# Selective-scan and attention kernel: five residual parts, stores over two blocks, one lasting tile for the scans of two states

## The chip, the cores and the metric

The kernel runs on one core of a Trainium2 chip. The metric is the device time of one execution in microseconds (us), the median of three runs. TensorE is called PE in the profile, VectorE DVE, ScalarE ACT, GpSimd POOL; SP is the SyncE queue, which issues DMAs only. ACT and POOL issue DMAs as well as computing.

## The reference, cut to what matters

There are 16 images of 128 channels by 64x64 positions, thus 4096 tokens each. Layer 0 is a selective scan with two channel halves of 128 and 16 states:

```python
def step(hs, inp):                      # over the 4096 tokens of an image
    d_t, B_t, C_t, u_t = inp
    dA = jnp.exp(d_t[:, :, None] * A)
    h_new = dA * hs + (d_t * u_t)[:, :, None] * B_t[:, None, :]
    y_t = jnp.einsum('bdn,bn->bd', h_new, C_t)
    return (h_new, y_t)
...
x = x + _L0_conv_ref(_gn(x), ...)       # the residual of layer 0
t = _to_tokens(x)
t = t + _L1_attn_ref(_ln_t(t), W_kv, q_proj)
t = t + _L1_ffn_ref(_ln_t(t), gate_w, gate_b, weight1, weight2)
```

Layer 0 has a grouped normalisation, an input projection, a causal convolution of four taps, the scan, a gate and an output projection; its result is added to its input `x`. Layer 1 has a causal attention with one query per head, and a mixture of experts.

## The kernel before, in words

**Blocks and steps.** An image is cut into 8 blocks of 512 tokens (`L = 512`, `NBLK = 8`). The first and longest stage is one loop over `k` (L804): iteration k runs the scan of block k, prepares block k+1 (normalise, convolution, projections, `delta`), finishes block k-1 (gate, output projection), and runs the attention of block m = k-9, nine blocks behind. Here i is the block's place in its image (0 to 7). An iteration has 16 steps, one for each state n (L873).

**What a step does.** DVE multiplies `bx = du * B` for both halves (`product`, two instructions), copies the last column of the scan of the step before into `state` (`keep_state`, one small reduction; left out in an image's last block), and runs the two scans (`scan`), each over 512 tokens. POOL multiplies the scan's result by C into `da` (`product_c`), one step behind DVE, and for n = 1, 3, 5, 7 issues a DMA that adds the product of the state before (`add_pair`, `da<-da`). PE sums the products in PSUM by transposes (`add_y`, names `y0` to `y13`; `yp14`, `yp15` run in the next iteration). SP loads `bct`, the rows of B and C spread to 128 partitions, three steps ahead (`load_bc`, five buffers). ACT makes the decays `da = exp(delta * a)` (`d`).

**The order written out by hand.** All else is placed by the table `STEP` (L749): for each step three lists of names, which run before the scans, between the two scans, and after them. Each engine executes its own instructions in that program order, and each engine issues its DMAs in its own order. The names that matter below: `k0`-`k7` and `v0`-`v7` are attention keys and values (a PE product, taken out by ACT with Silu); `s0`, `s1` scores on PE; `mx`, `l0`-`l5` the running maximum of the scores on DVE, `sexp` its exponential; `store` (ACT) writes the scores' logarithms to DRAM as `pd<-parts`, 96 KB in rows of 128 bytes, and `spread` (SP) reads them back in ten small DMAs (`lh<-pd`, `rh<-pd`), for the weights `w0`; `bcs` (ACT) stores B and C of the next block; `cen`, `sq`, `var`, `lnsc`, `la` are the token normalisation (`la` is DVE's `xn<-cen_ps,rstd`); `g0`, `g1` the gate on DVE (`z<-y_ps,z`); `gnl` loads and `gs` reduces a block of a later image (`stats<-xs`); `fin0`, `fin1` store the attention's result (`t_d<-tx`); `put` (ACT) copies a block of layer 0's result into `xt`, which holds one whole image (`res[b]`, one buffer).

**The residual.** When an image's last block has been put (iteration with i = 0 of the next image), POOL adds `x` to `xt` by DMA (`ar0`-`ar3`, `xt<-in_x_dram`, an accumulating DMA on POOL's queue), and ACT stores the sum to DRAM in quarters of 512 KB (`sr0`-`sr3`, `t_d<-xt`). The attention reads it from there block by block (`lx0`, `lx1`), but for the first block, which `cen` reads from `xt` directly.

After this loop come a gating stage, the experts and a final addition, which the change does not touch.

Of the kernel before, what the change touches and what calls it, by code (L numbers as in the profile page):

```python
# [8 lines left out]
F32 = mybir.dt.float32  # L9
BF16 = mybir.dt.bfloat16  # L10
AF = mybir.ActivationFunctionType
ALU = mybir.AluOpType
# [3 lines left out]
P = 128  # L16
L = 512
# [22 lines left out]
def bc(ap, shape):  # L40

    return ap.to_broadcast(list(shape))
# [3 lines left out]
def conv_attn_hybrid(ctx: ExitStack, tc: tile.TileContext, x, w_in, conv_w, conv_b, w_xproj, w_dt, b_dt,  # L46
                     a_log, d_param, w_out, w_kv, q_proj, gate_w, gate_b, weight1, weight2, out):
    nc = tc.nc
    NB, C, HH, WW = x.shape
    T = HH * WW  # L50
    NBLK = T // L
# [4 lines left out]
    NH2 = DI // P  # L56
# [11 lines left out]
    x_f = x.rearrange("b c h w -> b c (h w)")  # L68
# [19 lines left out]
    with ExitStack() as st:  # L88
# [5 lines left out]
        PE, DVE, ACT, POOL, SP = (InOrder(tc, e) for e in (nc.tensor, nc.vector, nc.scalar, nc.gpsimd, nc.sync))  # L94
# [131 lines left out]
        mp = st.enter_context(tc.tile_pool(name="mp", bufs=2))  # L226
        m1 = st.enter_context(tc.tile_pool(name="m1", bufs=1))
        dap = st.enter_context(tc.tile_pool(name="dap", bufs=13))
        hp_ = st.enter_context(tc.tile_pool(name="hp", bufs=2))
        bcp = st.enter_context(tc.tile_pool(name="bcp", bufs=5))  # L230
        tmp = st.enter_context(tc.tile_pool(name="tmp", bufs=6))
        vp_ = st.enter_context(tc.tile_pool(name="vp", bufs=4))
# [5 lines left out]
        blocks, gn, res, att = {}, {}, {}, {}  # L238

        def load_exp():  # L240
            tc.keep_in_program_order(nc.scalar.preload_act_table_set(EXP_LN))  # L241
# [4 lines left out]
        def bank(name):  # L246
            return ps.tile([P, L], F32, tag="ps", name=name)
# [16 lines left out]
        def gn_end(b, part):  # L264

            w = gn[b]
            if part == 0:
                w["mv"] = stp.tile([P, 2], F32, tag="mv", name="mv")
                w["gs"] = stp.tile([P, 5], F32, tag="gs", name="gs")
                DVE.bn_aggr(w["mv"], w["stats"].rearrange("p a b -> p (a b)"))  # L270
            mv, gs = w["mv"], w["gs"]
            if part == 1:
                w["gp"] = bank("gn_ps")
                PE.matmul(w["gp"][:, 0:1], gmat, mv[:, 0:1], start=True, stop=True)
                ACT.copy(gs[:, 0:1], w["gp"][:, 0:1])
            if part == 2:
                far = w["gp"][:, 1:2]
                DVE.tensor_tensor(far, mv[:, 0:1], w["gp"][:, 0:1], ALU.subtract)
                DVE.scalar_tensor_tensor(gs[:, 1:2], far, far, mv[:, 1:2], ALU.mult, ALU.add)
            if part == 3:  # L280
                w["gp"] = bank("gn_ps2")
                PE.matmul(w["gp"][:, 0:1], gmat, gs[:, 1:2], start=True, stop=True)
                ACT.activation(gs[:, 2:3], w["gp"][:, 0:1], AF.Ln, bias=eps)
                ACT.activation(gs[:, 3:4], gs[:, 2:3], AF.Exp, scale=-0.5)
            if part == 4:
                DVE.tensor_scalar(gs[:, 4:5], gs[:, 0:1], gs[:, 3:4], -1.0, ALU.mult, ALU.mult)
# [22 lines left out]
        def conv(k, a, taps=range(KC)):  # L309

            w = blocks[k]
            if taps[0] == 0:
                w[f"xs{a}"] = bank("xs_ps")
            pt = w[f"xs{a}"]
            for t in taps:
                PE.matmul(pt, wc[:, t, bass.ts(a, P)], w["xb"][:, t : t + L], start=(t == 0), stop=(t == KC - 1))
# [79 lines left out]
        def scan(k, n, between):  # L396


            w = blocks[k]
            b, i = w["b"], w["i"]  # L400
            if n == 0 and i == 0:
                gn[b]["state"] = stp.tile([P, N, NH2], F32, tag="state", name="state")
            bt, da, bx = w.pop(("bc", n)), w["da", n], w.pop("bx")
            h = w["h", n] = hp_.tile([P, NH2, L], F32, tag="h", name="h")
            for a in range(NH2):
                if a:
                    between(n)
                DVE.tensor_tensor_scan(h[:, a, :], da[:, a, :], bx[a],
                                       0.0 if i == 0 else gn[b]["state"][:, n, a : a + 1], ALU.mult, ALU.add)
            w["hc", n] = bt  # L410
# [15 lines left out]

        def keep_state(k, n):
            w = blocks[k]
            h = w.pop(("h", n))
            if w["i"] < NBLK - 1:  # L430
                DVE.tensor_reduce(gn[w["b"]]["state"][:, n, :], bc(h[:, :, L - 1 :], [P, NH2, 2]),
                                      mybir.AxisListType.X, ALU.max)

        def add_y(k, n):

# [39 lines left out]

        def add_residual(b, part):

            cols = (slice(0, L), slice(L, 2 * L), slice(2 * L, 4 * L), slice(4 * L, T))[part]
            for a in range(cols.start, cols.stop, 4 * L):
                to = slice(a, min(a + 4 * L, cols.stop))  # L480
                POOL.dma_start(res[b][:, to], x_f[b, :, to], accum_op=ALU.add)

        def store_residual(b, part):
            ACT.dma_start(t1_d[b, :, bass.ts(part, T // 4)], res[b][:, bass.ts(part, T // 4)])
# [152 lines left out]
        def split(m, part):  # L637
            s = att[m]
            ACT.copy(s["parts"][:, part], s["rest"][:, :P].rearrange("p (w s) -> p w s", s=64))
# [99 lines left out]
        def finish(m, f):  # L739
# [7 lines left out]
        PAIRS = (1, 3, 5, 7)  # L747
        LEAD, LEAD_BC = 8, 3
        STEP = (  # L749
# [16 lines left out]
        )  # L766
        order = [(k, n) for k in range(NK) for n in range(N)]
        made = 0
# [35 lines left out]
        for k in range(NK + LAG + 1):  # L804
            b, i = divmod(k, NBLK)
            cur = k if k < NK else None
            prev = k - 1 if 0 <= k - 1 < NK else None
# [9 lines left out]
                norm=(nxt, norm_block), conv0=(nxt, lambda k: conv(k, 0)), conv1=(nxt, lambda k: conv(k, 1, range(KC // 2))),  # L817
                conv2=(nxt, lambda k: conv(k, 1, range(KC // 2, KC))), csilu=(nxt, conv_silu), xproj=(nxt, xproj),
                bcs=(nxt, store_bc), delta=(nxt, delta), z=(cur, gate_silu), skip=(cur, skip),
                
                outp=(prev, out_proj), put=(prev, put_back),
                cen=(mn, ln_center), sq=(mn, ln_square), var=(mn, ln_var), lnsc=(mn, ln_scale), 
                mx=(m, score_max), sexp=(m, score_exp), tsc=(m, turn_scores), ssum=(m, score_sum),
                ssp=(m, spread_scores), slog=(m, score_log), rest1=(m, lambda m: rest(m, 1)), split1=(m, lambda m: split(m, 1)),
                rest2=(m, lambda m: rest(m, 2)), split2=(m, lambda m: split(m, 2)), store=(m, store_parts),
                spread=(m, spread_parts), inv=(m, inverse), lx0=(mn, lambda m: load_x(m, True)), lx1=(m, load_x),
                gnl=(stat, lambda s: gn_load(*s)),
                lb=(k + 2 if k + 2 < NK else None, lambda k: load_block(k, ACT)),
                nt=(k + 2 if k + 2 < NK else None, no_tokens), exp=(0, lambda _: load_exp()))
# [27 lines left out]
                ops[f"yp{n}"] = (prev, lambda k, n=n: add_y(k, n))  # L857
            for part in range(5):
                ops[f"ge{part}"] = (ends, lambda b, part=part: gn_end(b, part))
            for part in range(4):  # L860
                ops[f"ar{part}"] = (b - 1 if i == 0 and prev is not None else None, lambda b, part=part: add_residual(b, part))
                ops[f"sr{part}"] = (b - 1 if i == 0 and prev is not None else None, lambda b, part=part: store_residual(b, part))

            def do(n, part):
                for name in STEP[n][part].split():
# [34 lines left out]
    with ExitStack() as st:  # L900
        PE, DVE, ACT, POOL, SP = (InOrder(tc, e) for e in (nc.tensor, nc.vector, nc.scalar, nc.gpsimd, nc.sync))
# [17 lines left out]
        gn = rp_.tile([E, C], F32, name="gn", bufs=1)  # L919
# [145 lines left out]
        for it in range(NIT + LATE + 2):  # L1065
            p, i = divmod(it, NBLK)
# [22 lines left out]
            last, left = divmod(it - LATE - 2, NBLK)  # L1089
# [6 lines left out]
    with ExitStack() as st:  # L1096
# [3 lines left out]
        hp = st.enter_context(tc.tile_pool(name="hp", bufs=2))  # L1100
# [7 lines left out]
        for e0 in range(0, E, EG):  # L1108
            w1 = wpool.tile([P, EG, HID], F32, tag="w1", name="w1")
# [17 lines left out]
            ops = ps.tile([P, O], F32, tag="ops", name="ops")  # L1127
# [12 lines left out]
    with ExitStack() as st:  # L1140
        ps = st.enter_context(tc.tile_pool(name="cps", bufs=4, space=PSUM))
        cp = st.enter_context(tc.tile_pool(name="cp", bufs=2))
        for pr in range(NB // 2):
# [4 lines left out]
            for j in range(2):  # L1148
                b = 2 * pr + j
                t = cp.tile([P, T], F32, tag=f"t{j}", name=f"tc{j}")  # L1150
# [34 lines left out]
```

## Time and profile before

| | us |
|---|---|
| median of 3 runs | 9472.11 (9468.96 to 9473.5) |
| the profiled execution | 9471.73 |
| its span, first to last instruction | 9470.0 |
| busy: PE / DVE / ACT / POOL | 8291.2 / 8447.0 / 7282.9 / 5899.4 |
| DVE scans, 4096 of 512 columns | 4993.5 |
| DVE products `bx`, 4096 | 2652.0 |
| DVE `state<-h`, 1792 | 283.1 |
| mean granted TensorE clock | 0.933 |

The profile shows one execution. A group's row ends with: count | busy us, mean ns of one | idle time of that engine just before them, and what ended it. A row of waits has: who waited <- for what: us in total, times, longest. A row of a timeline has: start, length, engine, line, operation, count, and in brackets the idle time before it. Line 37 is the helper through which all instructions of the loop pass, so groups are told apart by the names of their tiles. Buffer numbers are left out. Rows of DMAs on POOL's queue carry a time to landing; on SP's and ACT's queues they do not, and landings there are read from what waited for them. Neighbouring DVE instructions overlap in the timeline: an instruction's length reaches some 0.1 us past the start of the next one.

### The profile page before, as it was taken

Reading aid. Unit: us, or ns where it says so; the run is one execution under the profiler, and the core shown is the slowest. Engines: PE = TensorE matmul, PEld = TensorE weight load, DVE = VectorE, ACT = ScalarE, POOL = GpSimd, SP = SyncE. Lnnn points to the kernel's source line nnn. Section 1 sums busy time; section 2 is a strip of 40 time slices with the busy share of each in tenths; the row PEclk is TensorE's granted clock in tenths of the full one; section 3 lists DMA queues with packets and bytes.
Section 4 is the critical chain, followed back from the end, with each engine's and each line's share of the span. In section 5 each row is a group of like instructions: output and inputs, shape, how many; then the busy total and the mean of one; then the engine's idle time right before and its main releaser. Section 6 shows DMA issues by size and latency. Waiting matters only on the chain.

```text
span 9470.0 us, 189268 instructions
## 1 busy us (share of the span) xinstructions
PE 8291.2 (88%) x69596; PEld 5233.9 (55%) x69596; DVE 8447.0 (89%) x13057; ACT 7282.9 (77%) x13950; POOL 5899.4 (62%) x2683
## 2 busy tenths in 40 slices
PE   5679999999989999999999999999999999877775
PEld 3446555555555565555555555555565555545642
DVE  8999999999999999999999999999999999603733
ACT  5568888888888888888888888888888888755730
POOL 6777777777777777777777777767777777500000
PEclk7789999999999999999999999999999999998976
DMA  6777877778777777777877777777877777502358
GB/s 173 184 201 189 202 193 201 191 196 204 189 203 193 201 189 203 192 198 197 201 191 196 200 190 202 195 197 190 202 194 199 197 196 189 147 22 71 113 183 358
DMA packets 978050, 1783.75 MB, mean 188 GB/s; under 512 B 194953, under 2 KB 275489, under 8 KB 967905
## 3 DMA queue, kind: packets, MB, share of 16 engines
q1 hardware_dynamic: 715264, 1347.76, 51.2%
q0 software_dynamic: 82944, 302.03, 16.2%
q10 hardware_dynamic: 178912, 121.86, 4.1%
q8 instruction: 548, 8.98, 0.4%
q14 instruction: 382, 3.12, 0.1%
HBM read 1363.99 MB, written 138.94 MB: 159 GB/s over the span
## 4 chain that ended last, share of the span: by engine, by line
PE 34%; ACT 20%; DMA 17%; DVE 15%; issue 8%; POOL 5%; SPq 1%; ACTq 0%; POOLq 0%; DVEq 0%
DVE h L37 8%; ACT da L37 7%; PE k_ps L37 6%; DMA da<-da 6%; PE y_ps L37 5%; PE v_ps L37 5%; POOL da L37 5%; DMA bct<-bcs 5%; PE ao_ps L37 4%; DVE bx L37 4%; PE xs_ps L37 3%; DMA pd<-parts 3%; PE s_ps L37 2%; ACT L37 2%; DMA xs<-in_x_dram 2%
## 5 line engine op out<-in xcount | busy, mean ns | idle before, releaser
L37 POOL TENSOR_TENSOR da<-h,bct 128x1024 f32<-128x1024 f32 x2048 | 5432.5, 2653 | 2155.8 <-DVE bx L37 1249.7
L37 DVE TENSOR_TENSOR_SCAN h<-da,state,bx 128x512 f32<-128x512 f32 x3584 | 4398.3, 1271 | 0.0
L37 DVE TENSOR_TENSOR bx<-du,bct 128x512 f32<-128x512 f32 x4096 | 2652.0, 698 | 60.4 <-DMA bct<-bcs 60.3
L37 ACT ACTIVATE da<-delta,a_neg 128x512 f32<-128x512 f32 x4096 | 2610.4, 717 | 15.4 <-DMA bct<-bcs 7.5
L37 PE MATMUL y_ps<-ident,da 128*128 128x128 f32 x12288 | 1698.8, 293 | 383.6 <-POOL da L37 219.2
L37 PEld LDWEIGHTS y_ps<-ident,da 128*128 128x128 f32 x12288 | 1515.1, 152 | 593.9 <-POOL da L37 257.8
L37 PE MATMUL v_ps<-wv,xn 128*64 128x512 f32 x4096 | 1032.4, 610 | 37.9 <-ACT tx L37 28.8
L37 ACT ACTIVATE v<-v_ps 128x512 f32<-128x512 f32 x1024 | 613.9, 600 | 526.4 <-PE v_ps L37 388.9
L37 PE MATMUL xs_ps<-xb,wc 128*128 128x512 f32 x2048 | 967.8, 606 | 2.5 <-issue 1.8
L37 PE MATMUL k_ps<-xn,wk 128*128 128x512 f32 x2048 | 951.1, 607 | 0.0
L37 ACT ACTIVATE kt<-k_ps 128x512 f32<-128x512 f32 x1024 | 612.6, 598 | 340.8 <-PE k_ps L37 270.7
L37 PEld LDWEIGHTS k_ps<-xn,wk 128*128 128x128 f32 x2048 | 369.6, 190 | 488.4 <-issue 435.4
L37 PE MATMUL ao_ps<-v,wm 128*64 128x128 f32 x8192 | 578.2, 285 | 54.9 <-ACT wm L37 54.8
L37 DVE TENSOR_TENSOR_SCAN h<-da,bx 128x512 f32<-128x512 f32 x512 | 595.2, 1203 | 0.0
L37 PEld LDWEIGHTS ao_ps<-v,wm 128*64 128x64 f32 x8192 | 451.7, 140 | 222.1 <-ACT wm L37 82.4
L37 POOL DMA_DIRECT2D da<-da x512 | 449.3, 878 | 163.4 <-POOL da L37 153.4
L37 PEld LDWEIGHTS xs_ps<-xb,wc 128*128 128x128 f32 x2048 | 368.2, 195 | 326.7 <-issue 325.7
L37 ACT ACT_TABLE_LOAD x397 | 509.4, 1283 | 21.6 <-issue 8.6
L37 PEld LDWEIGHTS v_ps<-wv,xn 128*64 128x64 f32 x4096 | 245.7, 136 | 480.3 <-issue 220.4
L37 PE MATMUL dt_ps<-dbl,wdt 8*128 8x256 f32 x1024 | 248.4, 446 | 139.3 <-ACT v L37 132.2
L241 ACT ACT_TABLE_LOAD x278 | 356.7, 1283 | 5.3 <-ACT tx L37 0.4
L37 PE MATMUL ao_ps<-v,e 128*32 128x128 f32 x8192 | 338.0, 284 | 0.0
(209 smaller groups left out, 10164.8 us busy)
## 6 DMA issues: line engine op xcount, KB each, us to landing
bct<-bcs SPq DMA_DIRECT2D x2048, 512.0 KB
da<-da POOLq DMA_DIRECT2D x512, 512.0 KB, 7.8
xs<-t_d SPq DMA_DIRECT2D x240, 256.0 KB
xs<-in_x_dram SPq DMA_DIRECT2D x128, 256.0 KB
t_d<-xt ACTq DMA_DIRECT2D x64, 512.0 KB
t_d<-tx ACTq DMA_DIRECT2D x256, 128.0 KB
t<-t_d SPq DMA_DIRECT2D x128, 256.0 KB
tc<-t_d SPq DMA_DIRECT2D x16, 2048.0 KB
```

The costliest lines, as they stand in the source:

```text
L37: return lambda *args, **kw: self.tc.keep_in_program_order(f(*args, **kw))
L241: tc.keep_in_program_order(nc.scalar.preload_act_table_set(EXP_LN))
```

## The change

Three things change.

1. The two rotating tiles `h` become the two halves of one lasting tile `hh`; scan n writes half n % 2. The copy of the last columns runs once for two states (after odd n), over four columns instead of two.
2. The residual is added in five parts instead of four: 1, 1, 2, 2, 2 blocks' columns instead of 1, 1, 2, 4. They stand at steps 8 (after the scans), 10, 12, 13 and 15, where they stood at 8, 9, 10 and 11. The first store, `sr0`, stands at step 14 of the iteration with i = 0, the others at steps 0, 3 and 4 of the iteration with i = 1; before, all four stood at steps 12 to 15 of i = 0.
3. Many other entries of `STEP` move by up to one step.

```diff
-        hp_ = st.enter_context(tc.tile_pool(name="hp", bufs=2))
+        hp_ = st.enter_context(tc.tile_pool(name="hp", bufs=1))
+        hh = hp_.tile([P, 2, NH2, L], F32, name="hh")
...
-            h = w["h", n] = hp_.tile([P, NH2, L], F32, tag="h", name="h")
+            h = w["h", n] = hh[:, n % 2]
...
-            h = w.pop(("h", n))
-            if w["i"] < NBLK - 1:
-                DVE.tensor_reduce(gn[w["b"]]["state"][:, n, :], bc(h[:, :, L - 1 :], [P, NH2, 2]),
-                                      mybir.AxisListType.X, ALU.max)
+            w.pop(("h", n))
+            if n % 2 and w["i"] < NBLK - 1:
+                last = hh.rearrange("p n a t -> p (n a) t")[:, :, L - 1 :]
+                DVE.tensor_reduce(gn[w["b"]]["state"][:, n - 1 : n + 1, :].rearrange("p n a -> p (n a)"),
+                                  bc(last, [P, 2 * NH2, 2]), mybir.AxisListType.X, ALU.max)
...
-            cols = (slice(0, L), slice(L, 2 * L), slice(2 * L, 4 * L), slice(4 * L, T))[part]
-            for a in range(cols.start, cols.stop, 4 * L):
-                to = slice(a, min(a + 4 * L, cols.stop))
-                POOL.dma_start(res[b][:, to], x_f[b, :, to], accum_op=ALU.add)
+            to = (slice(0, L), slice(L, 2 * L), slice(2 * L, 4 * L), slice(4 * L, 6 * L), slice(6 * L, T))[part]
+            POOL.dma_start(res[b][:, to], x_f[b, :, to], accum_op=ALU.add)
...
         STEP = (
-            ("ge0 yp14 yp15 v6 k0", "", "k4 k1 k2"),
-            ("k3", "k5", ""),
-            ("norm tu0 g0 fin0 ge1 g1", "", "s0"),
-            ("", "", "k6 k7 skip ty0 s1 ty1"),
-            ("v7 v4 lx0 mx v5 exp w1 y-1 d d ge2 l0 d d l1 l2", "l4", "d y1 ge3 conv0 l3 l5 d"),
-            ("sexp a10 outp d", "a11", "put tsc y3"),
-            ("ssp", "d", ""),
-            ("ssum slog conv1 ts1 rest1 d c1 split1 conv2 b1 rest2 csilu d", "", ""),
-            ("split2", "store ar0 lx1 z v2 ge4 to1 xproj v0 tu1", ""),
-            ("bcs", "ar1", ""),
-            ("cen fin1 v3 d sq v1 delta var y5", "exp ar2", ""),
-            ("ar3 lnsc y7 inv", "", "lb nt spread"),
-            ("sr0 y8 w0 d d", "", "y9 d"),
-            ("a00 a01 y10", "ts0 sr1 y11", "d c0 d y12"),
-            ("gnl sr2", "", "d la"),
-            ("y13 b0 gs", "d to0", "sr3"),
+            ("v6 ge0 yp14 sr1 k0 yp15 k1", "", "k2"),
+            ("k3 ge1 k4 k5", "", "tu0 norm g0"),
+            ("g1", "", "fin0"),
+            ("", "s0", "lx0 k6 k7 sr2 skip ty0 s1 v4"),
+            ("v5 sr3 v7 mx exp l0 d w1 ge2 ty1 y-1 d l1 d", "l2", "y1 l4 d conv0 d l3 l5 outp d"),
+            ("a10 ge3 sexp", "", "put a11 tsc"),
+            ("ssp d", "d", "ts1 y3"),
+            ("ssum slog conv1 rest1 d c1 d lx1 split1 conv2 csilu rest2", "", "split2 b1"),
+            ("", "store xproj z ge4", "ar0"),
+            ("to1 v2 bcs", "", "v3 tu1 v0 cen fin1 d"),
+            ("sq v1 y5 delta", "exp", "ar1 var lnsc"),
+            ("y7 inv", "", "lb"),
+            ("spread ar2 y8 w0 d d", "y9", "nt d"),
+            ("a00 y10 a01 ar3", "ts0 y11", "d gnl c0 d y12"),
+            ("", "sr0", ""),
+            ("b0 ar4 y13 d la d", "", "to0 gs"),
         )
...
-            for part in range(4):
-                ops[f"ar{part}"] = (b - 1 if i == 0 and prev is not None else None, ...)
-                ops[f"sr{part}"] = (b - 1 if i == 0 and prev is not None else None, ...)
+            for part in range(5):
+                ops[f"ar{part}"] = (b - 1 if i == 0 and prev is not None else None, ...)
+            for part in range(4):
+                ops[f"sr{part}"] = (b - 1 if i == (part > 0) and 0 < b <= NB else None, ...)
```

More of the change, by code (lines that the diff above doesn't have):

```diff
@@ L859, in conv_attn_hybrid @@
                 ops[f"ge{part}"] = (ends, lambda b, part=part: gn_end(b, part))
+            for part in range(5):
+                ops[f"ar{part}"] = (b - 1 if i == 0 and prev is not None else None, lambda b, part=part: add_residual(b, part))
             for part in range(4):
-                ops[f"ar{part}"] = (b - 1 if i == 0 and prev is not None else None, lambda b, part=part: add_residual(b, part))
-                ops[f"sr{part}"] = (b - 1 if i == 0 and prev is not None else None, lambda b, part=part: store_residual(b, part))
+                ops[f"sr{part}"] = (b - 1 if i == (part > 0) and 0 < b <= NB else None, lambda b, part=part: store_residual(b, part))
             def do(n, part):
```

## The prediction

> **What bounds the kernel now.** I read the page first, then the DVE and ACT waits of the loop's steady part, then windows of single blocks, then timelines around the places that the change touches.
>
> The page's first line, and the DVE groups with shapes kept apart:
>
> ```profile
> PE 8291.2 (88%) x69596; PEld 5233.9 (55%) x69596; DVE 8447.0 (89%) x13057; ACT 7282.9 (77%) x13950; POOL 5899.4 (62%) x2683
> ...
> L37 DVE TENSOR_REDUCE state<-h 128x2 f32<-128x4 f32 x1792 | 283.1, 158 | 0.0
> ```
>
> The 89% is an average over stages. Two windows, one over an iteration with i = 0 and one over an ordinary iteration, give busy time of PE, PEld, DVE, ACT, POOL, then the granted clock, DMA share, GB/s:
>
> ```profile
> 1551.40:1624.10 72.70, 61.43 (x516) 38.26 (x515) 61.83 (x92) 54.09 (x103) 49.14 (x24) 0.91 0.78 201
> 1687.30:1750.00 62.70, 58.12 (x502) 36.50 (x501) 62.49 (x93) 52.85 (x101) 45.54 (x20) 0.97 0.74 193
> ```
>
> An ordinary iteration is DVE work without a hole: 62.49 of 62.70 us, PE 58.12, ACT 52.85. In the i = 0 iteration DVE has 10.9 us of holes. From the starts of the first `bx` of each block: iterations with i = 2 to 5 take 62.81 us, i = 7 61.86, and i = 0 from the second image with attention on (14 of them) 72.03 on average, the first one with it 65.43. The DVE waits between 1088 and 7744 us, 13 images, name the holes:
>
> ```profile
> DVE xn L37 <- ACT rstd L37: 61.9, 15, 7.2
> DVE bx L37 <- DMA bct<-bcs: 50.7, 26, 5.0
> DVE stats L37 <- DMA xs<-in_x_dram: 21.1, 17, 3.2
> DVE mx L37 <- PE s_ps L37: 10.4, 12, 1.8
> ```
>
> The first three make 133.7 us, 10.3 for an image, nearly all at steps 14 and 15 of i = 0. So the time is DVE's instructions plus one stall an image.
>
> **Part 1: 1792 small reductions become 896.** All are on the path; the question is what one costs. The DVE timeline, a step without and a step with it:
>
> ```profile
> 1551.47 1.27 DVE L37 TENSOR_TENSOR bx<-du,bct 128x512 f32<-128x512 f32 x2
> 1552.66 2.32 DVE L37 TENSOR_TENSOR_SCAN h<-da,bx 128x512 f32<-128x512 f32 x2
> 1554.90 1.27 DVE L37 TENSOR_TENSOR bx<-du,bct 128x512 f32<-128x512 f32 x2
> 1556.08 0.15 DVE L37 TENSOR_REDUCE state<-h 128x2 f32<-128x4 f32 x1
> 1556.15 2.32 DVE L37 TENSOR_TENSOR_SCAN h<-da,bx 128x512 f32<-128x512 f32 x2
> ```
>
> From `bx` to scan it is 1.19 us without and 1.25 with it: 60 ns, not the row's 158. Whole iterations agree: i = 7 holds one reduction where the others hold 16, and is 0.95 us shorter, 63 ns each. Gain: 896 x 63 ns = 56 us. Each of the 896 that stay covers eight inputs instead of four; the set-up's reduction of eight inputs (`negc<-ident`) took 162 ns against 158, so +4 ns, 3.6 us. Net -53 us; bounds -56 (no growth) to -26 (each larger one 34 ns dearer in pitch).
>
> The Trainium skill, "VectorE: DVE Perf Modes", section "The DRAIN you can't avoid", says that the next instruction starts only when the pipe is empty. By that rule a removed reduction would free its whole 158 ns, 142 us in all; here the scan starts 70 ns after the reduction did, so the sum goes by 63.
>
> The lasting tile: scan n+1 writes the half that POOL's product of n-1 read, as before with two buffers. That a tile's parts are tracked apart is seen on `xt`, where the four accumulating DMAs, issued 3 us apart, were in flight together. So 0; if it did not hold, see the rivals.
>
> **Part 2: the stall of i = 0.** ACT around it, and SP's wait in the same iteration:
>
> ```profile
> 1590.49 0.38 ACTq L37 DMA_DIRECT2D pd<-parts  x1
> ...
> 1607.08 0.34 ACTq L37 DMA_DIRECT2D t_d<-tx  x1
> 1607.47 0.60 ACT L37 ACTIVATE v<-v_ps 128x512 f32<-128x512 f32 x1 [8.82 <-DMA pd<-parts]
> ...
> SPq L37 <- DMA pd<-parts: 13.4, 1, 13.4
> ```
>
> `pd` takes 16.6 us from issue to what it releases; in the next iteration 5.7 (1663.24 to 1668.97). In those 16 us all residual parts were in flight, 2 MB in POOL's queue: issued 1586.28, 1589.15, 1593.19, 1596.66, landed 1595.45, 1597.62, 1602.60, 1607.88. The late `pd` holds two queues. ACT's stands 8.8 us, so `rstd` and DVE's `xn` are late. SP's stands 13.4 us, so `bct` of state 15 goes out at 1610.37 instead of about 1600. What DVE then waits for:
>
> ```profile
> 1605.63 1.30 DVE L37 TENSOR_TENSOR bx<-du,bct 128x512 f32<-128x512 f32 x2 [1.84 <-DMA bct<-bcs]
> ...
> 1614.77 0.69 DVE L37 TENSOR_TENSOR xn<-cen_ps,rstd 128x512 f32<-128x512 f32 x1 [5.54 <-ACT rstd L37]
> ...
> 1621.37 0.69 DVE L37 BATCH_NORM_STATS2 stats<-xs 128x6 f32<-128x512 f32 x1 [3.20 <-DMA xs<-in_x_dram]
> ```
>
> After the change part 0 goes out as before (right behind POOL's product of state 7), part 1 one step later (about 1593), parts 2 to 4 at about 1600, 1604 and 1611. While `pd` is on its way only part 0's tail and part 1's beginning are there. I put `pd` between 5.7 and 16.6 us, near the low end, since there too one accumulating DMA was in flight (the pair sum, 1659.79 to 1667.15): 7 us, landing 1597.5. SP's ten small DMAs then took 4.7 us (1668.99 to 1673.7), so `bct` of 15 goes out at 1602, 8 us earlier. It took at most 5.2 us to its use (1610.37 to 1615.54), and 12.3 for the one caught between parts (1593.27 to 1605.63); with part 2 beside it I take 6.5: 1608.7. DVE without stalls needs it at 1607.2 (step 13 began at 1600.23, two steps of 3.49). That leaves 1.5 us; `la`, now behind `du`, and `gs`, now behind the scans, have 2 to 3 us more room each. With 1 us for what I overlook, 2.5 us remain of 10.6: -8.1 x 14 and -2.5 for the mild first image, together -116 us. Bounds: everything gone, 62.81 - 16 x 0.12 = 60.9 us for i = 0 (scans that start from a constant have steps of 3.49 instead of 3.61), -11.1 x 14 - 4.5 = -160; or parts 2 to 4 catch `bct` as parts 2 and 3 do now, 1597.5 + 4.7 + 12.3 = 1614.5, a stall of 7.3, -49; with `pd` still 16.6 us late as well, 0 to +10.
>
> The fifth issue costs POOL 0.9 to 1.5 us an image, in a queue that idles about 1 us a step: 0. The skill's "DMA: Bandwidth & Descriptors", section "Anatomy of one DMA", speaks against splitting: each such DMA pays a fixed 2 us (its figure). Nothing waits for the fifth part, so by the rule the sum would stay the same; the rows here have 8.9 us to landing for 256 KB, 9.0 for 512 and 11.0 for 1024.
>
> **Part 3: stores over two blocks.** At i = 1 ACT issues `sr1` in front of `k0`, `sr2` in front of `ty0`, `sr3` behind `v5`; one issue took 0.33 to 1.59 us. Queued behind them are keys, then scores, then DVE's `mx`. `mx` has 0.96 us to spare in an ordinary iteration (scores end 1640.14, `mx` starts 1641.10). I take +0.5 us x 15 = +8; bounds 0 and +30. `put`, which now waits for `sr3` in the single `xt`, comes about 12 us after it; the stores of before were issued until 1626.2, and DMA traffic on their queue had ended by 1631.
>
> **Part 4: the other moves.** Each keeps its place in its engine's queue to within a few instructions. `g0` comes 1.2 us earlier, with 3 to 4 us to spare; `yp15` moves behind `v6` and `k0`, filling the 0.73 us that PE waited for POOL there; `lx1` moves in front of `bct` of state 10 on SP, and needs PE's `a10`, done near 1652, when that load goes out (1652.30); `l4` moves behind the second scan, a few tens of ns either way. Sum 0; if the 0.96 us at `mx` were lost, every iteration would pay (below).
>
> **Sum.** 9471.7 - 53 - 116 + 8 = 9311 us for the profiled execution, which lies 0.4 us under the median of the runs. Forecast 9311.
>
> **Rivals.**
> A, the forecast: 0.60, own range 9255 to 9375.
> B, the stall stays, since `pd` meets part 0 and the pair sum anyway and `bct` of 15 meets parts 2 and 3: 9471.7 - 53 + 8 = 9427, 9400 to 9450. For it: `bct` has only 5 us between `pd`'s landing with spreading and its use. Against it: three of four parts move out of `pd`'s way. 0.22.
> C, slower: a DMA issue on ACT in front of `k6` (`fin0`'s `t_d<-tx`, step 2) waits for another DMA's end. Such waits exist (`ACT tx <- DMA bct<-bcs`: 63.3 us in 34 of 104 blocks, up to 3.9), and the order of issues changes. A wait of 3.9 us less the 0.96 to spare, in 112 blocks, costs 330: 9640. It turns the sign once the wait exceeds about 2.4 us in every block (161 us / 112 + 0.96). Against it: in the timelines that I read it strikes only at `fin1`, where DVE does not feel it. 0.11.
> D, the change doesn't do what it says: the lasting tile is tracked as a whole, and each scan waits for POOL's product of the step before, which ends 3.5 us into the step where scans start at 1.25: +2.2 x 2048 = 4.6 ms, 14.1 ms. 0.03.
> The rest, 0.04, is a mixture near no change.
>
> **Chances and range.** Runs of this kernel can tell some 0.2%, 19 us. Faster: A, B, and a little of the rest, 0.83; same 0.03; slower, C and D, 0.14. The range 9255 to 9450 holds A and B.
>
> **What would show it.** 896 reductions near 162 ns; ordinary iterations 0.4 to 0.5 us shorter; ACT's wait behind `pd` at i = 0 gone, `xn <- rstd` near 0, what is left on `bx <- bct` at step 15; `mx` waits little changed. Wrong if `mx`, `bx` or scans wait in every iteration, or if i = 0 still takes 70 us.

## The result, and the profile after

The changed kernel takes 9473.56 us (median of 12 runs, 9451.11 to 9498.29) beside 9473.87 for the kernel before (12 runs): a ratio of 0.9999, 95% interval 0.9989 to 1.0009. No change, where 9311 us was forecast. The profiled execution took 9474.06 us, its span 9472.0.

Two effects of about 100 us each cancel. From the first `bx` of block 0 to that of block 127 the profile has 8107.5 us instead of 8100.7. The iterations with i = 0 got shorter by 95 us in sum (72.04 to 65.55 us each in the 14 images, 65.43 to 61.06 in the first one with attention), and all others got longer by 102: an ordinary one takes 63.68 us instead of 62.81 (medians over i = 2 to 5).

The same two windows as before, an i = 0 iteration and an ordinary one (length, then busy PE, PEld, DVE, ACT, POOL, clock, DMA share, GB/s):

```profile
1566.40:1630.80 64.40, 60.76 (x538) 38.05 (x537) 61.58 (x84) 56.50 (x108) 50.21 (x25) 1.00 0.79 203
1758.50:1822.20 63.70, 59.95 (x503) 36.34 (x501) 62.69 (x86) 52.71 (x102) 46.00 (x20) 0.95 0.77 189
```

DVE's hole at i = 0 shrank from 10.9 to 2.8 us. In the ordinary iteration DVE runs 86 instructions instead of 93 and still is busy for 62.69 us, and a hole of 1.0 us has opened. The DVE waits between 1088 and 7744 us no longer have `xn <- rstd`:

```profile
DVE bx L37 <- DMA bct<-bcs: 41.5, 29, 5.8
DVE z L37 <- PE y_ps L37: 10.8, 12, 1.9
DVE stats L37 <- DMA xs<-in_x_dram: 9.4, 9, 2.0
```

SP's wait for `pd` in the i = 0 iteration, 13.4 us before, is down to:

```profile
SPq L37 <- DMA pd<-parts: 2.9, 1, 2.9
```

The new hole is too finely cut to lead such a list. It stands in the idle column of the DVE groups with shapes kept apart. The scans before:

```profile
L37 DVE TENSOR_TENSOR_SCAN h<-da,state,bx 128x512 f32<-128x512 f32 x3584 | 4398.3, 1271 | 0.0
L37 DVE TENSOR_TENSOR_SCAN h<-da,bx 128x512 f32<-128x512 f32 x512 | 595.2, 1203 | 0.0
```

And after, the scans and the reduction (the rows name what ended only a few of these gaps, each of which is short):

```profile
L37 DVE TENSOR_TENSOR_SCAN hh<-da,state,bx 128x512 f32<-128x512 f32 x3584 | 4394.5, 1265 | 77.2 <-DVE state L37 1.5 <-ACT da L37 1.5 <-ACT parts L37 0.5
...
L37 DVE TENSOR_TENSOR_SCAN hh<-da,bx 128x512 f32<-128x512 f32 x512 | 596.8, 1205 | 10.9 <-DVE state L37 0.5
...
L37 DVE TENSOR_REDUCE state<-hh 128x4 f32<-128x8 f32 x896 | 138.3, 154 | 0.0
```

The timeline shows what it follows. An even step with the reduction, an odd one without it, and step 2, where the gate stands behind the reduction:

```profile
1885.85 1.29 DVE L37 TENSOR_TENSOR bx<-du,bct 128x512 f32<-128x512 f32 x2
1887.05 0.16 DVE L37 TENSOR_REDUCE state<-hh 128x4 f32<-128x8 f32 x1
1887.34 2.45 DVE L37 TENSOR_TENSOR_SCAN hh<-da,state,bx 128x512 f32<-128x512 f32 x2
1889.70 1.28 DVE L37 TENSOR_TENSOR bx<-du,bct 128x512 f32<-128x512 f32 x2
1890.89 2.45 DVE L37 TENSOR_TENSOR_SCAN hh<-da,state,bx 128x512 f32<-128x512 f32 x2
...
1895.04 0.16 DVE L37 TENSOR_REDUCE state<-hh 128x4 f32<-128x8 f32 x1
1895.11 0.68 DVE L37 TENSOR_TENSOR z<-y_ps,z 128x512 f32<-128x512 f32 x1
```

A scan behind the reduction starts 0.29 us after the reduction did; the gate, and every scan of the kernel before, 0.07 us. Medians of the steps' lengths over i = 2 to 5: steps 8, 10, 12 and 14 take 3.84 us each where 8, 10 and 12 took 3.609 (+0.23), odd steps such as 3, 7 and 9 3.547 (-0.062). With 6 such gaps in an ordinary iteration, 6 x 0.23 - 8 x 0.062 = +0.88 us, and the iteration got 0.87 longer. In an image with attention there are 41 (step 0 of i = 1 to 7 but for i = 6, where another instruction lies between, and steps 6, 8, 10, 12 and 14 of i = 0 to 6); the trace has 665 scans that follow a reduction directly, which makes some 153 us.

**Theory T1:** at an even step n the scan writes half 0, whose last column the reduction has read just before. The two rotating tiles had no such pair of neighbours: the reduction read one tile, the scan wrote the other. So the scan now waits for the reduction's end, and its whole length and a wait of 0.13 us come onto DVE's path (88.1 us of idle in the two rows after the change, over 665 scans). That the scans of i = 0 wait too, which start from a constant and do not read `state`, speaks for the half and against `state` as the cause. The trace's semaphores agree: all 665 of these scans wait, among others, for the semaphore that DVE's own instructions count up, and of the 1457 scans that follow a reduction directly in the kernel before none does. So the wait is one that the program itself asks for. Rivals: the moved order (T0), the larger reduction (T2), and a lasting tile tracked as a whole (T3).

### The profile page after: what moved, and what is told of

The parts are those of the page before. It is cut to its first block, busy times and chain, and to the rows that moved or that the text cites. A ratio compares the mean times of both kernels' runs of the same rounds, so it can differ in the third digit from the quotient of the medians.

```text
span 9472.0 us, 187772 instructions
## 1 busy us (share of the span) xinstructions
PE 8324.7 (88%) x69596; PEld 5146.9 (54%) x69596; DVE 8455.5 (89%) x12161; ACT 7262.0 (77%) x13948; POOL 5947.9 (63%) x2699
## 4 chain that ended last, share of the span: by engine, by line
PE 44%; ACT 19%; DVE 14%; DMA 13%; issue 7%; POOL 3%; SPq 0%; ACTq 0%; DVEq 0%; POOLq 0%
PE ao_ps L37 8%; DMA da<-da 8%; PE y_ps L37 7%; DVE hh L37 7%; ACT da L37 6%; PE v_ps L37 6%; PE xs_ps L37 5%; PE k_ps L37 4%; DVE bx L37 4%; POOL da L37 3%; PE o_ps L37 2%; PE z_ps L37 2%; ACT e L37 2%; PE s_ps L37 2%; ACT L37 1%
## 5 line engine op out<-in xcount | busy, mean ns | idle before, releaser
L37 POOL TENSOR_TENSOR da<-hh,bct 128x1024 f32<-128x1024 f32 x2048 | 5439.7, 2656 | 2115.8 <-DVE bx L37 1178.0
L37 DVE TENSOR_TENSOR_SCAN hh<-da,state,bx 128x512 f32<-128x512 f32 x3584 | 4394.5, 1265 | 77.2 <-DVE state L37 1.5
L37 PE MATMUL y_ps<-ident,da 128*128 128x128 f32 x12288 | 1758.6, 292 | 396.9 <-DMA da<-da 261.3
L37 PEld LDWEIGHTS y_ps<-ident,da 128*128 128x128 f32 x12288 | 1487.8, 150 | 865.2 <-issue 367.0
L37 PE MATMUL v_ps<-wv,xn 128*64 128x512 f32 x4096 | 1026.1, 610 | 18.9 <-DVE gs L37 15.7
L37 PE MATMUL xs_ps<-xb,wc 128*128 128x512 f32 x2048 | 1011.9, 629 | 22.6 <-ACT wm L37 20.4
L37 DVE TENSOR_TENSOR_SCAN hh<-da,bx 128x512 f32<-128x512 f32 x512 | 596.8, 1205 | 10.9 <-DVE state L37 0.5
L37 PE MATMUL s_ps<-kt,q 128*32 128x64 f32 x16384 | 319.1, 221 | 5.2 <-ACT kt L37 4.1
```

Of the source, the lines that this page charges most:

```text
L37: return lambda *args, **kw: self.tc.keep_in_program_order(f(*args, **kw))
```

## The experiments

The ordinary iteration is the median over i = 2 to 5 with attention, i = 0 the mean of 14 images, `pd` the median time in i = 0 from its issue to the first read of it. Each ratio is to the kernel before, timed beside it.

| kernel | us (median) | ratio, 95% | ordinary | i = 0 | pd |
|---|---|---|---|---|---|
| before | 9473.87 | | 62.81 | 72.04 | 16.7 |
| after | 9473.56 | 0.9999 (0.9989 to 1.0009) | 63.68 | 65.55 | 5.1 |
| e1 pair alone | 9561.42 | 1.0097 (1.0084 to 1.0110) | 63.66 | 71.59 | 17.1 |
| e2 the rest alone | 9389.94 | 0.9913 (0.9900 to 0.9927) | 62.84 | 65.38 | 5.7 |
| e5 lasting, single | 9399.08 | 0.9927 (0.9912 to 0.9942) | 62.84 | 65.25 | 5.3 |
| e7 single, late | 9772.08 | 1.0318 (1.0302 to 1.0334) | 65.69 | 72.01 | 12.3 |
| e4 between | 9354.30 | 0.9876 (0.9863 to 0.9889) | 62.36 | 65.77 | 5.3 |
| e8 between, du twice | 9336.14 | 0.9854 (0.9840 to 0.9868) | 62.17 | 64.78 | 5.3 |
| e6 residual alone | 9417.81 | 0.9941 (0.9929 to 0.9954) | 62.81 | 66.84 | 6.3 |
| e9 adds back | 9422.86 | 0.9945 (0.9932 to 0.9957) | 62.36 | 70.86 | 15.7 |

### e1 and e2: each half of the change alone

e1 is the kernel before with the tile and the reduction of the change:

```diff
+        hh = hp_.tile([P, 2, NH2, L], F32, name="hh")
-            h = w["h", n] = hp_.tile([P, NH2, L], F32, tag="h", name="h")
+            h = w["h", n] = hh[:, n % 2]
...
+            if n % 2 and w["i"] < NBLK - 1:      # keep_state as in the change
```

> The kernel before with the lasting tile and the reduction for two states alone; order table and residual as before. Theory T1 (the scan after a reduction overwrites the columns that the reduction has just read, so it waits for the reduction's end): at steps 0, 6, 8, 10, 12 and at 14 the scan starts 285 to 300 ns after the reduction instead of 67, ordinary iterations are 62.81 - 8 x 0.06 + 6 x 0.23 = 63.7 us, i = 0 stays at about 73, and the time is about 9570 us. Rival T0 (the wait comes from the moved order, not from the tile): ordinary iterations 62.3 and about 9420 us.

It took 9561.42 us and its ordinary iteration 63.66: the reduction for two states, meant to save, costs 0.97%. Its idle columns are those of the changed kernel:

```profile
L37 DVE TENSOR_TENSOR_SCAN hh<-da,state,bx 128x512 f32<-128x512 f32 x3584 | 4390.4, 1264 | 77.5 <-DVE state L37 1.9 <-ACT e L37 1.0 <-ACT sq L37 0.5
L37 DVE TENSOR_TENSOR_SCAN hh<-da,bx 128x512 f32<-128x512 f32 x512 | 596.3, 1204 | 10.6
```

e2 is the changed kernel with the old tile pool and the old `keep_state` put back.

> The changed kernel with the two rotating tiles and one reduction for each state as before; residual and order table as changed. T1: no gap after any reduction, ordinary iterations 62.8 us, i = 0 about 65, and about 9375 us. T0 (the moved order costs): ordinary iterations stay above 63.3 us and about 9450 us or more.

It took 9389.94 us, 0.87% under the kernel before, with ordinary iterations of 62.84: the moved order costs an ordinary iteration nothing. T0 falls. The two halves, +0.97% and -0.87%, add up to nothing, as the whole did.

### e5: lasting tile, one small reduction a state

```diff
-            if n % 2 and w["i"] < NBLK - 1:
-                last = hh.rearrange("p n a t -> p (n a) t")[:, :, L - 1 :]
-                DVE.tensor_reduce(gn[w["b"]]["state"][:, n - 1 : n + 1, :]..., bc(last, [P, 2 * NH2, 2]), ...)
+            if w["i"] < NBLK - 1:
+                DVE.tensor_reduce(gn[w["b"]]["state"][:, n, :], bc(h[:, :, L - 1 :], [P, NH2, 2]), ...)
```

> The changed kernel with the lasting tile kept, but one reduction for each state as before, each reading the half that the next scan does not write. T1: no gap, as in the kernel with rotating tiles: ordinary iterations 62.8 us, about 9375 us. Rival T3 (a lasting tile is tracked as a whole, so any scan waits for any reader of it): the gap of 0.23 us comes after all 16 reductions, ordinary iterations 66 us or more, about 9800 us.

The gap is gone, and with it the idle time before the scans:

```profile
L37 DVE TENSOR_TENSOR_SCAN hh<-da,state,bx 128x512 f32<-128x512 f32 x3584 | 4390.2, 1265 | 0.6
L37 DVE TENSOR_TENSOR_SCAN hh<-da,bx 128x512 f32<-128x512 f32 x512 | 595.2, 1201 | 0.0
L37 DVE TENSOR_REDUCE state<-hh 128x2 f32<-128x4 f32 x1792 | 271.4, 151 | 0.0
```

9399.08 us is e2's time within the intervals, some 24 us above what was expected. T3 falls: a lasting tile costs nothing as such.

### e7: small reductions, each read just ahead of the overwrite

```diff
-                    keep_state(*divmod(k * N + n - 1, N))
+                    if k * N + n > 1:
+                        keep_state(*divmod(k * N + n - 2, N))
```

This stands in the kernel before, on the lasting tile: at step n the small reduction reads half n % 2, which scan n then overwrites.

> The kernel before, with the lasting tile and one small reduction for each state, but run one step later, so that at every step the scan overwrites the half that the reduction right before it has read. T1 (the wait is for a reader of the half to be overwritten, whatever the reduction's size): the gap of 0.23 us comes at 13 of 16 steps (not at 2, 4 and 15, where another instruction lies between), ordinary iterations 62.81 + 13 x 0.23 = 65.8 us, about 9800 us. Rival T2 (the reduction over four columns is what waits): no gap, 62.8 us, 9470 us.

```profile
1888.99 0.15 DVE L37 TENSOR_REDUCE state<-hh 128x2 f32<-128x4 f32 x1
1889.28 2.45 DVE L37 TENSOR_TENSOR_SCAN hh<-da,state,bx 128x512 f32<-128x512 f32 x2
1891.65 1.28 DVE L37 TENSOR_TENSOR bx<-du,bct 128x512 f32<-128x512 f32 x2
1892.83 0.15 DVE L37 TENSOR_REDUCE state<-hh 128x2 f32<-128x4 f32 x1
1892.90 1.28 DVE L37 TENSOR_TENSOR z<-y_ps,z 128x512 f32<-128x512 f32 x2
```

The gap stands behind small reductions as well, 0.29 us from start to start, and not where the gate lies between. The ordinary iteration is 2.88 us longer than before (expected 13 x 0.23 = 3.0), the time 9772 (expected 9800). T2 falls; the price follows the number of such neighbours, 6 or 13.

### e4: the reduction between the two products

```diff
             for a in range(NH2):
+                if a and 0 < k * N + n:
+                    keep_state(*divmod(k * N + n - 1, N))
                 w["bxi", a] = DVE.tensor_tensor(bx[a], w["du"][:, a, :], w["bc", n][:, 0, :], ALU.mult)
...
                     product_c(*divmod(k * N + n - 1, N), behind)
-                    keep_state(*divmod(k * N + n - 1, N))
```

> The changed kernel with the reduction for two states put between the two products of its step, so that the second product (0.6 us) lies between it and the scan that overwrites what it read. T1: the wait is over before the scan comes up, gaps gone, ordinary iterations 63.68 - 6 x 0.23 = 62.3 us, about 9320 us, that is, the time that was forecast. Rival T2 (a reduction over four columns is itself dear, wherever it stands): ordinary iterations stay near 63.7 us and about 9470 us.

```profile
1887.40 0.68 DVE L37 TENSOR_TENSOR bx<-du,bct 128x512 f32<-128x512 f32 x1
1887.99 0.16 DVE L37 TENSOR_REDUCE state<-hh 128x4 f32<-128x8 f32 x1
1888.06 0.70 DVE L37 TENSOR_TENSOR bx<-du,bct 128x512 f32<-128x512 f32 x1
1888.66 2.45 DVE L37 TENSOR_TENSOR_SCAN hh<-da,state,bx 128x512 f32<-128x512 f32 x2
```

The same 896 reductions now cost 0.07 us of pitch each, and the idle time before the scans is gone:

```profile
L37 DVE TENSOR_TENSOR_SCAN hh<-da,state,bx 128x512 f32<-128x512 f32 x3584 | 4393.8, 1266 | 0.6
```

The ordinary iteration takes 62.36 us, as expected. The time, 9354.30, is 34 us above what was expected. The `bx <- bct` waits between 1088 and 7744 us rose from 41.5 to 59.3 us, but in e8, which is faster still, they are 42.7; where the 34 us went stays open. This version beats both kernels, by 1.24%.

### e8: the same wait elsewhere

e4 with `du` in a pool of two buffers: `du = w["du"] = mp.tile(...)` in place of `m1.tile(...)`.

> The kernel with the reduction between the two products, and du in two buffers instead of one. If T1 holds for any tile, the 0.2 us between the last product and du at step 15 (797 ns from start to start in the changed kernel, against 583 between two products) are the same wait, since du is overwritten right after a product has read it: they fall to about 0.6 us, 0.2 x 128 = 25 us, about 9330 us. Rival (du waits there for ACT's delta): no change, 9354 us.

```profile
1836.69 1.29 DVE L37 TENSOR_TENSOR bx<-du,bct 128x512 f32<-128x512 f32 x2
1837.88 1.23 DVE L37 TENSOR_TENSOR du<-delta,xc 128x1024 f32<-128x1024 f32 x1
```

From the last product to `du` it is 601 ns (median) instead of 797, the ordinary iteration 0.20 us shorter, the time 9336.14: the lowest median, 1.46% under the kernel before. The intervals of e4's and e8's ratios just overlap, so the shorter iteration is the firmer evidence. The rival, a wait of `du` for ACT's `delta`, falls: the second buffer alone took the delay away. The same two neighbours stood in the kernel before, 751 ns apart (median of the ordinary iterations).

### e6 and e9: what ended the stall of i = 0

e6 is the kernel before with only the residual changed (five parts, moved stores).

> The kernel before with the residual alone changed: five parts at steps 8, 10, 12, 13 and 15, stores at step 14 and at steps 0, 3 and 4 of i = 1; tile, reductions and all other entries as before. Theory R1 (the 2 MB that were in flight behind pd made the stall of i = 0): pd is released within 8 us, i = 0 falls from 72 to 65 to 67 us, ordinary iterations stay at 62.81, about 9385 us. Rival R0 (the other moved entries, la and gs above all, took the stall away): i = 0 stays above 70 us, about 9460 us.

`pd` fell from 16.7 to 6.3 us, `xn <- rstd` from 61.9 us to 1.2, i = 0 to 66.84 us; the time, 9417.81, is 33 us above what was expected. What was left:

```profile
DVE stats L37 <- DMA xs<-in_x_dram: 49.3, 19, 4.9
DVE bx L37 <- DMA bct<-bcs: 25.5, 16, 3.9
```

`gs` still stands ahead of step 15's scans here, and waits; behind them, as in the change, it waited 9.4 us. So R1 holds. e2, which has the other moves too, is 28 us below e6, so these carry that much together; how much of it is `gs`, no run shows.

e9 is e4 with the adds alone put back: four parts at steps 8, 9, 10 and 11, the stores as changed.

> The kernel with the reduction between the two products, with the residual's adds put back to four parts at steps 8, 9, 10 and 11; the stores stay over two iterations. R1: pd again takes about 16 us, i = 0 goes from 66 back to 70 or more, and the time rises by about 70 us to 9425. Rival R2 (the stores at the end of i = 0 made the stall, not the adds): i = 0 stays at 66 us, 9354 us.

```profile
DVE bx L37 <- DMA bct<-bcs: 131.1, 41, 7.8
```

`pd` is back at 15.7 us, i = 0 at 70.86, the time some 69 us over e4's. The stores, which stayed, are not the cause: R2 falls. With `la` later, the lateness now shows at `bx` alone instead of at `xn`. The sizes of the parts and their steps went back together, so which of the two counts was not separated.

The late `pd` is the usual way in which the adds hold SP, but not the only one. In one image of the kernel before (i = 0 from 6160.6 to 6234.0 us) SP began to read `pd` 5.2 us after its issue, and then stood 13.5 us before the fifth of the ten reads, waiting for a `bct` load that was in flight with the same parts; that iteration took 73.5 us, like its neighbours.

## Why the prediction was wrong, point by point

**Part 1, the reductions: wrong in sign, -53 us forecast, +90 measured (e1).** The step that failed is "the lasting tile: scan n+1 writes the half that POOL's product of n-1 read, as before with two buffers. ... So 0". It looked at the readers on other engines only. The reduction for two states reads both halves, also the one that the very next DVE instruction overwrites. What came in its place is a wait of the scan for the reduction, 0.29 us from start to start instead of 0.07, 665 times; the prediction's own sign of being wrong, "scans wait in every iteration", is what the trace shows. The sum had used the 60 ns between a reduction and a scan that have nothing in common, for a pair that has. The price of a pair with something in common was in the trace of before, at step 4, where a transpose reads what `mx` has just written:

```profile
1567.81 0.28 DVE L37 TENSOR_TENSOR_SCAN mx<-negc,s_ps 128x64 f32<-128x64 f32 x1
1568.19 0.23 DVE L37 STREAM_TRANSPOSE s_ps<-mx 128x32 f32<-128x32 f32 x1
```

0.28 us long, and 0.38 to the next start: its whole length and 0.10 more. By that row the larger reduction costs 0.16 + 0.10 = 0.26 instead of 0.067, which over 665 scans is +128 us, and the forecast would have been about 9440; the 26 us by which parts 2 and 3 fell short bring that to 9466. The rest of part 1 held: the larger reduction takes 154 ns (forecast 162), an odd step is 62 ns shorter (forecast 63), and where nothing waits (e4 against e2) the ordinary iteration is 0.48 us shorter.

The Trainium skill, "VectorE: DVE Perf Modes", section "The DRAIN you can't avoid", has the next instruction wait for the pipe to empty, and adds that "A next op that is not held starts earlier". The prediction set the first aside and left the second out. The runs show both, with the times beside them: 0.29 us for a scan that waits for the reduction's semaphore, 0.07 for one that doesn't. The same section reports eight copies that took as long with a semaphore after each as with one after the last, so that "the semaphore costs nothing extra here"; in this kernel the step from the one kind of pair to the other costs 0.23 us.

**Part 2, the stall: right in mechanism, too large in size.** `pd` takes 5.1 us (forecast 7), `xn <- rstd` is gone, what is left waits on `bct` and `stats` at step 15. Forecast with part 3: -108 us; e2 shows -82. Step 15's `bct` still comes late by more than the 2.5 us assumed for all: e2's i = 0 has 65.38 us, the forecast 63.9.

**Part 3, the stores: about right in size, by chance, and wrong in place.** e2's i = 1 is 64.27 us against 63.37, +0.9 where 0.5 was forecast; but `mx` waits no more, and `bct` does, at steps 1, 7 and 15 of i = 1, beside 1.5 MB of stores.

**Part 4, the other moves:** nearly right. Forecast was 0, and in e2 the iterations i = 2 to 7 of an image take 1.2 us more together. `g0`, said to have 3 to 4 us to spare, waits for `y_ps` now (10.8 us over 13 images), and `du` starts 46 ns later behind the last product.

**Rivals.** Of the worked cases B's time was nearest, for a reason that is not B's: the stall went. What C describes, a wait in every iteration that eats the gain, is what happened, and at the size that C gave for the turning point: 2.4 us less 0.96 to spare is 1.44, and 6 x 0.23 is 1.4. But it stands behind a DVE instruction, not behind a DMA issue on ACT. D was ruled out rightly (e5). The range ended below no change because part 1 had been given bounds of one sign only.

## What to carry to other kernels

Before merging or moving a small instruction on a full engine, look at what now stands right behind it on the same engine: if that overwrites or reads what the small one touches, the small one costs its whole length and a wait (here 0.29 us), and if not, a fraction of its length (0.07). Keep an unrelated instruction between the two, which here turned 9474 us into 9354, or use one more buffer, as e8 does for `du`. When a DMA of many small rows feeds the critical queue, try to keep large accumulating DMAs away until it has landed.

## What the runs showed of the hardware that was not expected

A DVE instruction that must wait for the one in front of it on the same engine started after that one's end: 0.13 us behind the reduction (0.29 from start to start), 0.10 behind `mx`, 0.03 (before) to 0.10 (after) for `du` behind `bx`. An unrelated one started before its end (0.07 from start to start). The delay came whether the first wrote what the second reads (`mx`) or read what the second overwrites (`hh`, `du`). Whether a scan could safely start earlier behind such a reduction was not tried.

`pd`, 768 rows of 128 bytes or only 96 KB, took 5.1 to 5.3 us beside a pair sum and the first two residual parts of 256 KB (after, e4), and 15.7 to 16.7 us where the larger parts were in flight with them (before, e9); these are medians, and single images of e9 have 8.8 to 17.8.

In the i = 0 iteration that the prediction shows, ACT stood 8.8 us before an issue (`t_d<-tx`) that does not touch `pd`. The trace shows why: in all 14 images of the kernel before, that issue counts the same completion semaphore as `pd` and waits for it first.
